# A two-layer transformer block on one core: layer 0's norms split, one key tile a step through DRAM, one copy per Strassen group, and output weight sums in product order

## The chip, the cores and the metric

One core of a Trainium2 chip runs the whole computation in one launch. The metric is the device time of that launch in microseconds (us). Engines: PE (TensorE, matrix products and transposes), DVE (VectorE), ACT (ScalarE), POOL (GpSimd) and SP (SyncE, which here issues nearly all DMAs). Each engine works through its own queue in order; semaphores tie the queues together.

## What is computed

Two layers over x (4 sequences of 256 tokens, 512 wide, fp32), each an attention and a feed-forward part, with a layer norm after each sum:

```python
x = _layernorm(x + _L0_attn_ref(x, ...))   # 32 query heads, 8 key/value heads, head size 16, causal, softmax, biases
x = _layernorm(x + _L0_ffn_ref(x, ...))    # x @ W.T + bias, W = scales * (codes - 128), 512 x 512
x = _layernorm(x + _L1_attn_ref(x, ...))   # 32 query heads, 8 key/value heads, head size 128, causal, bias -slope*sqrt(distance)
x = _layernorm(x + _L1_ffn_ref(x, ...))    # x @ w, w one block of 64 rows repeated 8 times
# _layernorm(x) = (x - mean) / sqrt(var + 1e-5)
```

## The kernel before, in words

Tokens lie in eight tiles of 128 (`tt`), two to a sequence. Both layers run the same software pipeline, `run` (L315): in each turn it begins a step (scores, softmax), calls `fill` (pieces of other work: projections, tails, output products), transposes the probabilities of the step begun `lag` turns earlier, and ends (products with v) the step begun `lag + more` turns earlier. The order within each engine's queue is made from this by a scheduler that places instructions by their dependences; `keep_in_program_order` and `issue_after` pin a few.

**Layer 0.** 64 steps: 4 sequences `b`, 2 query tiles `qt`, 2 groups `h` of key heads, 4 query groups `i`. The eight steps of a sequence with `qt` 0 have one key tile and are called its one-tile half, the eight with `qt` 1 have two key tiles and are its two-tile half. `begin0` (L453) multiplies 32-row slices of qT and kT into a score tile `sc` of two PSUM banks; two such tiles exist, so the scores of a step wait until the exponentials of the step two before have read theirs. DVE adds the causal mask (L467) and takes the negated maximum (L470), ACT makes four exponentials with their sums (L270), DVE takes the reciprocal (L275), and POOL divides (L276). `transpose0` (L483) turns the probabilities, so that keys are on partitions, in one of two ways:

- on PE (`transposed_probabilities`, L286): four 128x128 transposes into a PSUM bank for each key tile, then an ACT copy (L480) into `prT`;
- through DRAM (`transposed_by_blocks`, L294): DVE transposes 32x32 blocks (L300), SP writes them to a DRAM tile `way` with four DMAs (L306) and reads them back into `prT` with one (L310).

`BY_BLOCKS` chooses the steps of the second way, for all their key tiles at once: groups 0 and 2 of a one-tile half, groups 0 and 1 of a two-tile half, except for the one-tile half of sequence 0. `end0` (L501) multiplies with v once all four groups are there (L512). When both `h` are done, `tail0` (L418) is queued: output projection `py` (L422), sum (L424), `layer_norm` (L252: statistics on DVE, the power -0.5 on POOL at L259, the normalisation on DVE at L260), transposes `pt_x` (L266), feed-forward `pf` (L437), second norm, transposes into x2T. Each `yield` ends a piece that one `fill` emits.

**Layer 1.** 64 steps: 8 key/value heads `kv`, 4 sequences, 2 query tiles; lag 1, more 1. The projections (`project1`, L647) and the output products (`outputs1`, `output_products`) are in Strassen's form with seven products in place of eight: `Quarters.early` makes products 1 and 2, `late` the rest; the sums on the left and right sides are POOL's (`left_sums` L591, `right_of` L829). All products go through a ring of three PSUM banks (`bank_m`). `early` copies product 1 out twice:

```python
nc.scalar.copy(C[0, 0], bank)
nc.scalar.copy(C[0, 1], bank)
bank = self.product(2, A[0, 1], Bq[1, 0])
nc.vector.tensor_tensor(C[0, 0], bank, C[0, 0], ALU.add)
```

`output_products` (L894) runs once per head and sequence: product 4, then 1 and 5, 6 and 7, 2 and 3 (PE line L851). Probabilities go through DRAM, but for the last head, whose transposes are on PE and whose `prT` is written in plain order.

Of the kernel before, what the change touches and what calls it, by code (L numbers as in the profile page):

```python
# [59 lines left out]
def block_kernel(  # L60
# [190 lines left out]

    def layer_norm(dst, y, name):  # L252
        st = s0.tile([P, 6], F32, tag="bn", name=f"bn_{name}", bufs=4)
        mv = s0.tile([P, 2], F32, tag="mv", name=f"mv_{name}", bufs=4)
        rs = s0.tile([P, 1], F32, tag="rs", name=f"rs_{name}", bufs=4)
        nc.vector.bn_stats(st, y)
        nc.vector.bn_aggr(mv, st)
        nc.vector.tensor_scalar(rs, mv[:, 1:2], EPS, 1.0, ALU.add, ALU.mult)
        powers.append(nc.gpsimd.tensor_tensor(rs, rs, minus_half, ALU.pow))  # L259
        nc.vector.tensor_scalar(dst, y, mv[:, 0:1], rs, ALU.subtract, ALU.mult)  # L260

# [24 lines left out]
    def transposed_probabilities(name, pr, parts, copy=evacuate):  # L286

        for kt, dst in enumerate(parts):
            pt = bank_t(f"pt_{name}_{kt}")
            for i in range(G):  # L290
                nc.tensor.transpose(pt[:, i, :], pr[:, i, ts(kt, P)], ident)
            copy(dst, pt)

    def transposed_by_blocks(sp, name, pr, nt, dst, bufs):  # L294

        blocks = sp.tile([P, 2, 4, G, 32], F32, tag="blocks", name=f"blocks_{name}", bufs=bufs)
        for kt in range(nt):
# [118 lines left out]
    def tail0(tt, oT):  # L418
# [4 lines left out]
        y = s0.tile([P, D], F32, tag="y", name=f"y_{tt}")  # L423
        nc.vector.tensor_tensor(y, py, x[tt], ALU.add)  # L424
        x1 = s0.tile([P, D], F32, tag="x1", name=f"x1_{tt}")
        layer_norm(x1, y, f"a{tt}")
        yield True
        yield True
# [11 lines left out]
        y2 = s0.tile([P, D], F32, tag="y", name=f"y2_{tt}")  # L440
        nc.vector.tensor_tensor(y2, pf, x1, ALU.add)
        x2[tt] = xp.tile([P, D], F32, tag="x", name=f"x2_{tt}")
        layer_norm(x2[tt], y2, f"b{tt}")
        yield True
        yield True
# [30 lines left out]
    open0 = {}  # L476
    BY_BLOCKS = [(0, 2), (0, 1)]

    def ordered_copy(dst, src):
        nc.scalar.copy(dst, src.rearrange("p n (j q) -> p n j q", q=32))  # L480


    def transpose0(b, qt, h, i, pr):  # L483

        name = f"0_{b}_{qt}_{h}_{i}"
        nt = qt + 1
        if i == 0:
            open0["p", h] = a0.tile(
                [P, 2, G, 4, 4, 32], F32, tag="prT", name=f"prT0_{b}_{qt}_{h}"
            )  # L490
        prT = open0["p", h]
        if (b, qt) > (0, 0) and i in BY_BLOCKS[qt]:
            transposed_by_blocks(a0, name, pr, nt, prT[:, 0:nt, i], 2)
        else:
            copy = evacuate if (b, qt) == (0, 0) else ordered_copy
            transposed_probabilities(
                name, pr, [prT[:, kt, i].rearrange("p j n q -> p n j q") for kt in range(nt)], copy
            )
        return prT
# [37 lines left out]
    def fill():  # L537
# [12 lines left out]
        lag=3,  # L550
        more=2,
    )
# [37 lines left out]

    def left_sums(S, A):  # L591
        nc.gpsimd.tensor_tensor(S[0], A[1, 0], A[1, 1], ALU.add)
        nc.gpsimd.tensor_tensor(S[1], S[0], A[0, 0], ALU.subtract)  # L593
        nc.gpsimd.tensor_tensor(S[2], A[0, 0], A[1, 0], ALU.subtract)
        return nc.gpsimd.tensor_tensor(S[3], A[0, 1], S[1], ALU.subtract)

    class Quarters:
# [15 lines left out]
        def early(self):  # L613

            A, C = self.A, self.C
            bank = self.product(1, A[0, 0], Bq[0, 0])
            nc.scalar.copy(C[0, 0], bank)
            nc.scalar.copy(C[0, 1], bank)  # L618
            bank = self.product(2, A[0, 1], Bq[1, 0])
            nc.vector.tensor_tensor(C[0, 0], bank, C[0, 0], ALU.add)  # L620
            yield True
# [206 lines left out]

    def right_of(kv):  # L829
        if kv not in rights:  # L830
            wo1 = weights1[kv][1]
            Bm = {
                (j, m): wo1[:, 2 * j : 2 * j + 2, ts(m, HALF)] for j in range(2) for m in range(2)
            }
            to = s1.tile([P, 3, 2, HALF], F32, tag="to", name=f"to_{kv}", bufs=1)
            T2_, T3_, T4_ = (to[:, n] for n in range(3))
            T1_ = Bm[0, 1]
            with tc.issue_after(powers[-1].ins):
                nc.gpsimd.tensor_tensor(T3_, Bm[1, 1], Bm[0, 1], ALU.subtract)
                nc.gpsimd.tensor_tensor(T1_, Bm[0, 1], Bm[0, 0], ALU.subtract)  # L840
                nc.gpsimd.tensor_tensor(T2_, Bm[1, 1], T1_, ALU.subtract)
                nc.gpsimd.tensor_tensor(T4_, Bm[1, 0], T2_, ALU.subtract)
            T = T1_, T2_, T3_, T4_
            rights[kv] = Bm, T
        return rights[kv]

# [36 lines left out]
    def outputs1(kv, b, o2):  # L883
        Bm, T = right_of(kv)
        A = {(l, j): o2[:, l, 2 * j : 2 * j + 2, :] for l in range(2) for j in range(2)}
        so = s1.tile([P, 4, 2, P], F32, tag="so", name=f"so_{kv}_{b}", bufs=1)
        S = [so[:, n] for n in range(4)]
        done = left_sums(S, A)
        if merges:
            with tc.issue_after(done.ins):  # L890
                merge()
        return output_products(kv, b, A, S, Bm, T)

    def output_products(kv, b, A, S, Bm, T):  # L894
        (S1, S2, S3, S4), (T1, T2, T3, T4) = S, T
        name = f"{kv}_{b}"
        flat = [kept[b][:, n].rearrange("p a n -> p (a n)") for n in range(2)]
        first = kv == 0
        bank = products(f"po4_{name}", [(A[1, 1], T4)])
        corner = x2[2 * b + 1][:, 0:HALF]  # L900
        nc.vector.tensor_tensor(corner, bank, corner, ALU.add)
        added(flat[0], products(f"po15_{name}", [(A[0, 0], Bm[0, 0]), (S1, T1)]), first)
        yield True
        added(flat[1], products(f"po67_{name}", [(S2, T2), (S3, T3)]), first)
        bank = products(f"po23_{name}", [(A[0, 1], Bm[1, 0]), (S4, Bm[1, 1])])
        nc.vector.tensor_tensor(x2[2 * b], bank, x2[2 * b], ALU.add)
        if kv == NKV - 2:
            merges.append(b)
        yield True

# [32 lines left out]
    def transpose1(kv, b, qt, pr):  # L943
        name = f"1_{kv}_{b}_{qt}"
        nt = qt + 1
        if kv == NKV - 1:
            prT = s1.tile([P, 2, 4, G, 32], F32, tag="prT", name=f"prT_{name}")
            transposed_probabilities(
                name, pr, [prT[:, kt].rearrange("p j h q -> p (j h q)") for kt in range(nt)]
            )  # L950
            return prT
        prT = s1.tile([P, 2, 4, G, 32], F32, tag="prT", name=f"prT_{name}")
        transposed_by_blocks(s1, name, pr, nt, prT[:, 0:nt], 1)
        return prT

    def end1(kv, b, qt, prT):
        o = ps_o.tile([P, G * P], F32, tag="o", name=f"o1_{kv}_{b}_{qt}")
        for kt in range(qt + 1):
            nc.tensor.matmul(  # L959
                o,  # L960
                v1[:, 2 * b + kt, ts(kv, P)],
                prT[:, kt].rearrange("p j h q -> p h j q")
                if kv < NKV - 1
                else prT[:, kt].rearrange("p j h q -> p (j h q)"),
                start=(kt == 0),
# [94 lines left out]
```

## Time and profile before

| What | Value |
| --- | --- |
| Three runs of the kernel | 987.88, 989.89, 992.61 us (median 989.89) |
| The profiled execution | 987.82 us, span 985.9 us |
| Mean granted TensorE clock | 0.980 |
| Busy: PE, DVE, POOL, ACT | 935.1, 620.6, 442.8, 327.3 us |
| First product of layer 1 (p_k, L610) | 294.7 us after the start of the span |
| PE busy, 0 to 300 us and 400 to 900 us | 267.06 of 300 and 493.66 of 500 us |
| DRAM trips: writes of 128 and 64 KB, reads | 176, 160, 84 |

How to read it: the span runs from the first to the last instruction of the core; the time of an execution is a little longer than its span. Rows name engine, line, operation, and out<-in with shapes; a number behind "idle" or in brackets with an arrow is the time that the engine stood before the instruction, and what released it. An fp32 product of the program is two PE instructions; 512 columns start every 0.43 us, 256 every 0.216, 128 every 0.109. PEclk is the share of the clock that PE was granted.

### The profile page before, as it was taken

What the parts mean: (1) busy time and instruction counts of PE and PEld (TensorE: products, weight loads), DVE (VectorE), ACT (ScalarE), POOL (GpSimd) and SP (SyncE); (2) the same over time, 40 slices, a digit from 0 to 9 for tenths busy, and PEclk for the clock granted to TensorE, in tenths of its full rate; (3) what the DMA queues carried; (4) which work ended last, traced back from release to release, by engine and by line L of the source; (5) the groups of instructions that cost most, each with busy time, mean ns of one, the idle gap of its engine ahead of it and who ended that gap; (6) DMA issues with size and microseconds to landing.
All of it is one profiled execution on the core that took longest, in us unless ns stands there. A gap on an engine that the chain in (4) does not pass through costs nothing.

```text
span 985.9 us, 11321 instructions
## 1 busy us (share of the span) xinstructions
PE 935.1 (95%) x3417; PEld 541.9 (55%) x3417; DVE 620.6 (63%) x1291; ACT 327.3 (33%) x1218; POOL 442.8 (45%) x461
## 2 busy tenths in 40 slices
PE   7999889988889999999999999999999999999996
PEld 5645435443334444566666666566666566657652
DVE  3786756766733445855666676566666566666566
ACT  2556454565522001423222222222222222223442
POOL 2364452553426512444543633634534553457732
PEclk9999979998899999999999999999999999999998
DMA  9444343443332010444433444333453434343001
GB/s 264 151 104 114 79 112 74 97 117 76 71 100 85 22 43 4 104 136 120 140 108 95 125 132 110 122 82 114 116 141 86 108 88 135 78 126 88 0 22 64
DMA packets 106817, 97.50 MB, mean 99 GB/s; under 512 B 8197, under 2 KB 77446, under 8 KB 106758
## 3 DMA queue, kind: packets, MB, share of 16 engines
q1 hardware_dynamic: 105942, 95.36, 35.9%
q10 hardware_dynamic: 816, 1.44, 0.5%
q8 instruction: 27, 0.44, 0.2%
q14 instruction: 32, 0.26, 0.1%
HBM read 61.11 MB, written 35.65 MB: 98 GB/s over the span
## 4 chain that ended last, share of the span: by engine, by line
PE 74%; POOL 8%; DVE 8%; ACT 5%; issue 2%; DMA 1%; SPq 0%; POOLq 0%; DVEq 0%; ACTq 0%
PE p_q L610 18%; PE po L851 14%; PE o L959 7%; PE sc L919 7%; PE p_v L610 5%; PE p_k L610 5%; POOL pr L276 4%; ACT pr L270 4%; PE o L512 3%; PE py L815 3%; PE sc L462 3%; DVE blocks L300 2%; PE pq L383 2%; DVE nm L470 2%; PE py L422 2%
## 5 line engine op out<-in xcount | busy, mean ns | idle before, releaser
L270 ACT ACTIVATE pr<-sc,nm 128x256 f32<-128x256 f32 (+1 forms) x512 | 209.0, 419 | 375.4 <-DVE nm L935 272.1
L276 POOL TENSOR_TENSOR pr<-pr,sums 128x512 f32<-128x512 f32 (+1 forms) x128 | 187.8, 1469 | 275.9 <-DVE sums L275 262.4
L300 DVE STREAM_TRANSPOSE blocks<-pr 128x512 f32<-128x512 f32 x128 | 87.5, 698 | 69.1 <-POOL pr L276 69.1
L927 DVE SCALAR_TENSOR_TENSOR sc<-table,sc 128x128 f32<-128x128 f32 (+1 forms) x256 | 86.2, 356 | 34.1 <-PE sc L919 32.1
L270 ACT ACTIVATION_READ_ACCUMULATOR pr<-sc,nm 128x1 f32 x512 | 103.6, 202 | 0.0
L919 PEld LDWEIGHTS sc<-kT,qT 128*128 128x128 f32 x512 | 82.1, 191 | 35.2 <-issue 28.7
L919 PE MATMUL sc<-kT,qT 128*128 128x256 f32 (+1 forms) x512 | 95.4, 327 | 0.0
L959 PE MATMUL o<-prT,v 128*128 128x512 f32 x192 | 92.9, 592 | 0.0
L625 DVE TENSOR_TENSOR qT<-p_q,qT 128x512 f32<-128x512 f32 x96 | 64.4, 685 | 34.1 <-PE p_q L610 33.4
L462 PE MATMUL sc<-kT,qT 32*128 32x256 f32 (+1 forms) x256 | 64.3, 564 | 11.8 <-ACT pr L270 11.6
L935 DVE TENSOR_REDUCE nm<-sc 128x2 f32<-128x512 f32 (+1 forms) x128 | 70.2, 551 | 1.7
L851 PE MATMUL po<-wo,o 128*128 128x256 f32 x224 | 58.0, 381 | 4.0 <-ACT qT L618 4.0
L470 DVE TENSOR_REDUCE nm<-sc 128x4 f32<-128x512 f32 (+1 forms) x64 | 60.6, 948 | 0.7
L610 PE MATMUL p_q<-x2T,ws_q 128*128 128x512 f32 x128 | 60.0, 592 | 0.0
L102 ACT COPY o<-o 128x512 f32<-128x512 f32 x29 | 17.0, 585 | 128.8 <-PE o L959 128.8
L610 PE MATMUL p_q<-xt,ws_q 128*128 128x512 f32 x128 | 57.8, 593 | 1.8 <-POOL ws_q L593 1.8
L467 DVE TENSOR_TENSOR sc<-sc,causal 128x512 f32<-128x512 f32 x64 | 43.9, 687 | 22.9 <-PE sc L462 22.6
L610 PE MATMUL p_q<-x2T,wq 128*128 128x512 f32 x128 | 57.6, 592 | 0.0
L851 PE MATMUL po<-wo,so 128*128 128x256 f32 x224 | 57.5, 379 | 0.0
L512 PE MATMUL o<-prT,v 128*32 128x512 f32 x192 | 53.0, 654 | 2.0 <-issue 2.0
L851 PE MATMUL po<-to,so 128*128 128x256 f32 x224 | 52.9, 379 | 0.0
L851 PEld LDWEIGHTS po<-to,so 128*128 128x128 f32 x224 | 42.6, 190 | 16.9 <-issue 12.2
(160 smaller groups left out, 1406.2 us busy)
## 6 DMA issues: line engine op xcount, KB each, us to landing
way<-blocks SPq DMA_DIRECT2D x176, 128.0 KB, 2.5
prT<-way SPq DMA_DIRECT2D x44, 512.0 KB, 3.7
way<-blocks SPq DMA_DIRECT2D x160, 64.0 KB, 1.8
prT<-way SPq DMA_DIRECT2D x40, 256.0 KB, 2.7
wq<-in_L_attn_w_qkv_dram SPq DMA_DIRECT2D x8, 1024.0 KB, 5.2
wo<-in_L_attn_w_o_dram SPq DMA_DIRECT2D x8, 1024.0 KB, 5.9
wk<-in_L_attn_w_qkv_dram SPq DMA_DIRECT2D x4, 512.0 KB, 4.4
wv<-in_L_attn_w_qkv_dram SPq DMA_DIRECT2D x2, 1024.0 KB, 5.1
```

The lines of the kernel that those rows point to most:

```text
L270: nc.scalar.activation(pr[:, i, 0:w], sc, AF.Exp, bias=nm[:, i : i + 1], accum_out=sums[:, i : i + 1])
L276: nc.gpsimd.tensor_tensor(pr[:, :, 0:w], pr[:, :, 0:w], sums.unsqueeze(2).to_broadcast([P, G, w]), ALU.mult)
L300: nc.vector.transpose(blocks[:, kt].rearrange("p j h q -> p h j q"), pr[:, :, ts(kt, P)].rearrange("p h (j k) -> p h j k", k=32),)
L462: nc.tensor.matmul(sc[:, j, :, 0:w], qT[rows, i, ts(qt, P)], kT[rows, :, 0:w], start=True, stop=True)
L470: nc.vector.tensor_reduce(nm, scf[:, :, 0:w], AX.X, ALU.max, negate=True)
L512: nc.tensor.matmul(o[32 * r : 32 * r + 32, :], v[:, kt, r, ts(e, 32)], prT[:, kt, :, :, 2 * j + e, :], start=(kt == 0 and e == 0), stop=(k ...
L610: nc.tensor.matmul(bank, fixed, moving, start=(c == 0), stop=(c == 1))
L851: nc.tensor.matmul(bank[:, ts(n, HALF)], left[:, c, :], right[:, c, :], start=(c == 0), stop=(c == 1),)
L919: nc.tensor.matmul(sc[:, m, 0:w], qT[:, 2 * j + m, b * S + qt * P : b * S + (qt + 1) * P], kT[:, b * S : b * S + w], start=True, stop=True,)
L927: nc.vector.scalar_tensor_tensor(sc[:, m, 0:w], table[:, 2 * P - w :], slopes[kv * G + 2 * j + m], sc[:, m, 0:w], ALU.mult, ALU.add,)
L935: nc.vector.tensor_reduce(nm[:, 2 * j : 2 * j + 2], sc[:, :, 0:w], AX.X, ALU.max, negate=True)
L959: nc.tensor.matmul(o, v1[:, 2 * b + kt, ts(kv, P)], prT[:, kt].rearrange("p j h q -> p h j q") if kv < NKV - 1 else prT[:, kt].rearrange(" ...
```

## The change

Five edits:

1. `layer_norm` is cut into `norm_factors` (statistics, power) and `normalise`; `tail0` has a `yield` between them, and one fewer behind.
2. Layer 0's probabilities: one key tile, tile 0, of a step goes through DRAM, for every step of the two-tile halves and the even groups of the one-tile halves; tile 1 goes through PE. Not in the one-tile half of sequence 0, nor in the last four steps (sequence 3, `qt` 1, `h` 1), which go through PE altogether. `blocks` is half as large there, with two buffers as before. `more` is 3 in place of 2.
3. `Quarters.early` copies product 1 once, and product 2 is added from that copy.
4. The output weight's four sums are issued between the left sums of the first sequence, and that sequence takes product 4 last.
5. The last head's `prT` is written in the order of the others.

```diff
-    def layer_norm(dst, y, name):
+    def norm_factors(y, name):
...
         powers.append(nc.gpsimd.tensor_tensor(rs, rs, minus_half, ALU.pow))
-        nc.vector.tensor_scalar(dst, y, mv[:, 0:1], rs, ALU.subtract, ALU.mult)
+        return mv[:, 0:1], rs
+
+    def normalise(dst, y, factors):
+        nc.vector.tensor_scalar(dst, y, *factors, ALU.subtract, ALU.mult)
...
-        for kt, dst in enumerate(parts):
+        for kt, dst in parts:
...
-            copy(dst, pt)
+            copy(dst, pt.rearrange("p i (j q) -> p i j q", q=32))
...
-    def transposed_by_blocks(sp, name, pr, nt, dst, bufs):
+    def transposed_by_blocks(sp, name, pr, nt, dst, room):
...
-        blocks = sp.tile([P, 2, 4, G, 32], F32, tag="blocks", name=f"blocks_{name}", bufs=bufs)
+        blocks = sp.tile(
+            [P, room, 4, G, 32], F32, tag="blocks", name=f"blocks_{name}", bufs=2 // room
+        )
...
+        factors = norm_factors(y, f"a{tt}")
+        yield True
         x1 = s0.tile([P, D], F32, tag="x1", name=f"x1_{tt}")
-        layer_norm(x1, y, f"a{tt}")
-        yield True
+        normalise(x1, y, factors)
         yield True
...
-    BY_BLOCKS = [(0, 2), (0, 1)]
...
-        if (b, qt) > (0, 0) and i in BY_BLOCKS[qt]:
-            transposed_by_blocks(a0, name, pr, nt, prT[:, 0:nt, i], 2)
-        else:
-            copy = evacuate if (b, qt) == (0, 0) else ordered_copy
...
+        rest = range(qt + 1)
+        if (0, 0) < (b, qt) and (b, qt, h) < (B - 1, 1, 1) and (qt == 1 or i % 2 == 0):
+            rest = rest[1:]
+            transposed_by_blocks(a0, name, pr, 1, prT[:, 0:1, i], 1)
+        copy = evacuate if (b, qt) == (0, 0) else nc.scalar.copy
+        transposed_probabilities(
+            name, pr, [(kt, prT[:, kt, i].rearrange("p j n q -> p n j q")) for kt in rest], copy
+        )
...
-        more=2,
+        more=3,
...
-    def left_sums(S, A):
+    def left_sums(S, A, between=None):
         nc.gpsimd.tensor_tensor(S[0], A[1, 0], A[1, 1], ALU.add)
+        if between:
+            between()
...
             bank = self.product(1, A[0, 0], Bq[0, 0])
-            nc.scalar.copy(C[0, 0], bank)
             nc.scalar.copy(C[0, 1], bank)
             bank = self.product(2, A[0, 1], Bq[1, 0])
-            nc.vector.tensor_tensor(C[0, 0], bank, C[0, 0], ALU.add)
+            nc.vector.tensor_tensor(C[0, 0], bank, C[0, 1], ALU.add)
...
+        less(T3_, Bm[1, 1], Bm[0, 1])
+        less(T1_, Bm[0, 1], Bm[0, 0])
+        yield True
+        less(T2_, Bm[1, 1], T1_)
+        yield True
+        less(T4_, Bm[1, 0], T2_)
+        yield True
...
+        if b == 0:
+            right = right_sums(kv)
+            next(right)
+            left_sums(S, A, lambda: next(right))
+            next(right)
...
+        order = [four, one_and_five, six_and_seven, two_and_three]
+        if b == 0:
+            order = order[1:] + order[:1]
+        for n, part in enumerate(order):
+            part()
+            if n == 3 and kv == NKV - 2:
+                merges.append(b)
+            if n % 2:
+                yield True
...
-                name, pr, [prT[:, kt].rearrange("p j h q -> p (j h q)") for kt in range(nt)]
+                name, pr, [(kt, prT[:, kt].rearrange("p j h q -> p h j q")) for kt in range(nt)]
```

## The prediction

> **What bounds the kernel now.** First the page: which engine is full where.
>
> ```profile
> span 985.9 us, 11321 instructions
> ...
> PE   7999889988889999999999999999999999999996
> ...
> DVE  3786756766733445855666676566666566666566
> ...
> POOL 2364452553426512444543633634534553457732
> PEclk9999979998899999999999999999999999999998
> ```
>
> A slice is 24.6 us. From slice 13 (320 us, layer 1) PE is full at full clock; in the first twelve (layer 0) it has gaps, and the granted clock dips exactly there. So layer 1 is priced by its few PE gaps, layer 0 by what starves PE. Next the windows by half sequence of layer 0 (columns: window, length, then busy us of PE, weight loads, DVE, ACT, POOL; then PEclk):
>
> ```profile
> 70.70:101.70 31.00, 30.61 (x142) 15.71 (x141) 21.84 (x46) 17.11 (x73) 13.59 (x13) 1.00 0.45 115
> 101.70:142.50 40.80, 34.21 (x137) 15.61 (x136) 28.68 (x51) 18.70 (x72) 18.59 (x14) 0.90 0.40 94
> 142.50:175.30 32.80, 32.75 (x140) 16.05 (x140) 20.13 (x44) 16.93 (x74) 12.26 (x12) 0.92 0.31 81
> 175.30:210.60 35.30, 30.79 (x135) 14.82 (x134) 27.37 (x49) 18.72 (x72) 18.75 (x14) 1.00 0.45 105
> ```
>
> The halves with one key tile (first, third) are full on PE. Those with two key tiles are not, though DVE is busy only 28 of 35 to 41 us: DVE, strictly in order, waits too. The timeline at 112 to 121 shows for whom:
>
> ```profile
> 112.14 1.30 DVE L300 STREAM_TRANSPOSE blocks<-pr 128x512 f32<-128x512 f32 x2 [0.90 <-POOL pr L276]
> ...
> 114.24 1.89 POOL L276 TENSOR_TENSOR pr<-pr,sums 128x1024 f32<-128x1024 f32 x1 [2.14 <-DVE sums L275]
> ...
> 116.09 0.55 POOL L259 TENSOR_TENSOR rs_b<-rs_b,minus_half 128x1 f32<-128x1 f32 x1
> 116.68 0.55 DVE L260 TENSOR_SCALAR x<-y,mv_b,rs_b 128x512 f32<-128x512 f32 x1 [0.92 <-POOL rs_b L259]
> ...
> 120.44 2.08 PE L462 MATMUL sc<-kT,qT 32*128 32x512 f32 x4 [3.45 <-ACT pr L270]
> ```
>
> A block transpose waits for POOL's divide (1.89 us after the reciprocal); the normalise waits for a power queued behind another divide. The next score's maximum is queued behind both, its exponentials come late, their PSUM banks come free late, and PE stands 3.45 us. Then the clock halves, as these windows (same columns) show:
>
> ```profile
> 116.90:120.40 3.50, 0.08 (x1) 0.00 (x0) 3.50 (x6) 1.93 (x8) 0.00 (x0) 0.99 0.01 4
> 120.40:127.10 6.70, 6.67 (x18) 1.83 (x18) 2.68 (x6) 2.41 (x9) 6.10 (x4) 0.50 0.67 157
> ```
>
> Such spells begin at 120, 141, 236 and 257 (6.8 us each) and two half as long at 32 and 274: 34 us, of which about 14 us are lost.
>
> In layer 1 a PE gap looks like this (timeline at 625):
>
> ```profile
> 625.47 1.89 PE L851 MATMUL po<-to,so 128*128 128x256 f32 x8
> ...
> 626.59 0.58 ACT L617 COPY qT<-p_q 128x512 f32<-128x512 f32 x1
> ...
> 627.96 0.61 ACT L618 COPY qT<-p_q 128x512 f32<-128x512 f32 x1
> ...
> 628.62 1.13 PE L851 MATMUL po<-wo,o 128*128 128x256 f32 x4 [1.26 <-ACT qT L618]
> ```
>
> The products need the bank that the second copy still reads.
>
> **The change, part by part.** Orders of the changed program are those in which it is built.
>
> *One copy per Strassen group.* 24 ACT copies of 0.59 us go. ACT is 33% busy, so their 14 us count only where they hold a bank. Eight product matmuls at 0.216 us from 625.47 end at 627.20, PE went on at 628.62: 1.42 us, and the first copy was done at 627.17. This stall appears twice (627, 780); a smaller one of 0.65 us three times (562, 715, 868). Gain 2.8 + 1.9 = 4.7.
>
> *Output weight's sums.* The source interleaves them with the left sums, but in the built POOL queue the four weight sums still stand together ahead of the left sums. What does change is PE: for the first sequence product 4 goes last. Before, it waited for the fourth weight sum (0.70 us, at 561, 713, 867); now product 1 starts at once, and product 5 waits for the first left sum (ending 562.3 by the old times, when PE would come at 561.9): 0.45 us. Gain 3 x 0.25 = 0.75, and most of 0.93 us at 412. Layer 1 in sum: **-6**, between 0 and -10 (PE's and its weight loads' waits for L618 and L842 sum to 15.7, but overlap). The last head group's probabilities are now written permuted: the ordered copy (0.594 us) costs what the plain one does (0.588): nothing.
>
> *One key tile a step.* In the two-tile half, four steps sent two tiles through DRAM and four none; now each of eight sends one. DVE's count is the same (8 x 0.70 us), PE's and ACT's too. What differs is the number of times that DVE waits for a divide. I walk DVE's queue of sequence 2's two-tile half from the end of the maximum of step 0 to that of step 7, each instruction at its row (causal 0.69, maximum 1.21, reciprocal 0.17, block 0.70, y, statistics 0.67 each, normalise 0.55; four exponentials 1.94 after the maximum; divide 1.99 after the reciprocal with its start; power 0.6 behind the divide). A wait is 1.99 less what stands between reciprocal and block. The old queue gives waits of 1.4, 0.8, 0.9, 0.95, 2.0, 0.6, in sum 6.6, and ends after 32.2 us; the trace has 31.5, so the walk can be trusted to a few per cent. The new queue: reciprocal and block stand side by side (2.0), around a maximum (0.85), a normalise behind a divide (1.2), a reciprocal right behind its maximum (1.65), around causal (1.3), around y (1.3), normalise (1.15): 9.45. So **+3** for each of three such halves, and +0.5 in the four DRAM steps left in the fourth: **+9.5** (behind the waiting block stand the next step's causal add and maximum on DVE; for them wait ACT's exponentials, then the score bank, then PE), from 0 (PE's order hides it) to +15 (each wait also starves PE).
>
> SP: 40 trips of five issues take the place of 28, 60 more issues at 0.44 us. A step then takes some 2.2 us of SP in a step of 4 to 5 us. The read of a trip now stands behind three writes of the next step, so its tile lands about 6 to 8 us after its transposes; the o products come three steps, some 13 us, later. Cost 0; without that cover some 2 us per o. In the two-tile halves an issue moves 64 instead of 128 KB and lands in 1.8 instead of 2.5 us.
>
> *more=3.* The o products come one step later. At 234.6 PE stood 2.14 us for a read issued at 233.89; that goes, and the half clock of 236.3 to 243.1 behind it: 2.1 + 2, **-4** (0 to -5.5). The probabilities' and v's buffers are held a step longer: two steps are left before they are wanted again, cost 0.
>
> *The end of layer 0.* The last four steps go through PE: four more tiles, 16 transposes of 0.109 us, 1.7 us, in place of DMA trips. From the last maximum (275.4) to layer 1's first product (294.7) the trace has 19.3 us: o waited for a read until 275.9, ran at half clock, the feed-forward, 16 transposes, then pt_x for a normalise (1.3 us), and only then the last o. In the new PE order the last o stands ahead of that pt_x. From the last maximum, at 29.8 us of the same walk: divide done 33.8; PE meanwhile does transposes, o (3.6), feed-forward (1.7), last transposes to 36.9, copy, o to 41.1, oT, py to 43.5. The trace took 51.0 over the same stretch: **-7.5** (-2 to -10).
>
> *Norms in two pieces.* The normalise moves behind one or two instructions; its wait for the power (3.9 us in all) stays, about 1 us each, as walked above: 0 (-5 to +3). pt_x waits of 1.8 to 1.9 us behind it stay as likely.
>
> *The clock.* The half-clock spells cost some 14 us of layer 0. I leave as many as there are, beyond the one above: 0, from -7 to +10.
> [...]
>
> **Sum.** -6 + 9.5 - 4 - 7.5 = -8 on the profiled 987.8 (span 985.9 and 1.9 around it): 979.8. The median of the runs, 989.9, is 2.1 above that execution, so I add part of it: **981**.
>
> **Rivals.**
> *DVE's waits decide (slower).* In the two-tile halves DVE's queue gets 36 us where PE needs 30. If the added waits fall together, as 1.2 + 1.65 do between steps 2 and 3, PE's gap passes 3 us, and each half gets two half-clock spells of 3.4 us cost: 3 halves x (3 + 4 to 5) = +23, less 6 and 7.5 elsewhere: 998. It decides from about one more spell per half. For it: the 3.45 us gap above. Against it: the window from 175.3 shows gaps of 1.5 to 1.9 us with PEclk 1.00.
> *Evening pays.* PE's own queue hides the new waits, stalls on the scores' banks (15 us in layer 0) shrink by half and with them half of the clock loss: -8 - 9.5 - 3 = 967. For it: DVE and PE have equal work in every step. Against: the walk.
> *Only layer 1 gains*, the end of layer 0 being eaten by the waits and a new spell: 988 in the median. It includes that the reordered sums do nothing, which the POOL queue suggests.
>
> **How the numbers follow.** The sum 0.50 (own range 974 to 988), DVE's waits 0.18, evening 0.20, layer 1 alone 0.12. A difference of 0.5% is about what can be told from no change here. Faster (under 985): 0.50 x 0.75 + 0.20 + 0.12 x 0.1, about 0.59; slower (over 994.8): 0.17; same: 0.24. The range runs from evening to most of the slow case: 965 to 997.
>
> **What would show it.** Right: no wait of po for an ACT copy; DVE's waits for the divide in the first 300 us up from 18.5 to about 28; layer 1 beginning 2 us sooner than 294.7; o in layer 0 never waiting for a read. Wrong: PEclk under 0.9 in more slices of layer 0, or the last o waiting for the last divide for over 4 us more than walked.

## The result, and the profile after

The changed kernel takes 992.98 us (median of 13 runs, 991.16 to 994.48), the kernel before 989.75 (13 runs, 985.06 to 992.61): ratio 1.0039, interval 1.0025 to 1.0053. It is slower, by less than 0.5%; forecast were 981 us and a range of 965 to 997. The profiled execution took 993.61 us, its span is 991.4. Two executions among the experiments below, one of e1 (1014.92 us) and one of g1 (1216.22 us), were slow, at a granted clock of 0.931 and 0.751, and are left out of the ratios and medians. The page of the changed kernel, same lines as before:

```profile
span 991.4 us, 11477 instructions
...
PE   7989979989989999999999999999999999999996
...
DVE  3757766656754345755566666667666666666566
...
POOL 2344443443444611443633534543544453467732
PEclk9889999989899999999999999999999999999998
```

PE is full from slice 13 on as before; the dips of PE and of the granted clock are still all in layer 0, but for the last slice (6 and 8). After the first slice the clock is under 0.9 in four slices of layer 0 (before: three), and PE is busy for under 90% in four (before: six). The stages say where the time came from. Layer 1 (first product to the end of the span) went from 691.2 to 688.5 us, layer 0 from 294.7 to 302.9. In layer 0 I cut at the end of the first maximum of each half sequence. Windows of the changed kernel, sequences 1 and 2, one-tile and two-tile half in turn (columns: window, length, busy us of PE, weight loads, DVE, ACT, POOL; PEclk; DMA share, GB/s):

```profile
82.10:114.10 32.00, 31.50 (x140) 15.13 (x139) 22.52 (x47) 16.30 (x74) 11.99 (x13) 1.00 0.39 100
114.10:153.10 39.00, 32.53 (x137) 16.75 (x134) 26.40 (x46) 18.87 (x69) 19.02 (x13) 0.91 0.36 90
153.10:187.00 33.90, 31.45 (x140) 15.04 (x138) 21.84 (x48) 16.68 (x76) 11.97 (x13) 1.00 0.36 90
187.00:227.40 40.40, 35.50 (x138) 16.82 (x134) 26.47 (x47) 18.91 (x69) 19.09 (x13) 0.84 0.33 82
```

The two-tile halves of sequences 1 and 2 in the kernel before, cut the same way:

```profile
108.00:145.10 37.10, 30.60 (x117) 13.96 (x117) 25.53 (x47) 18.93 (x71) 18.07 (x13) 0.85 0.42 100
179.30:212.80 33.50, 28.96 (x126) 14.00 (x128) 25.55 (x47) 18.85 (x71) 18.03 (x13) 1.00 0.50 121
```

The two-tile halves are now 39 and 40 us long where DVE is busy for 26 and POOL for 19, and part of PE's 33 and 36 busy us is there only because its clock was at 0.91 and 0.84. Cut the same way, the three two-tile halves of sequences 0 to 2 took 28.5, 37.2 and 33.5 us before and 35.0, 39.0 and 40.4 after: +15.2. The one-tile half of sequence 3 went from 30.9 to 27.7, the last half up to layer 1 from 51.0 to 47.8, the rest by -0.6: +8.2 in all for layer 0, -2.8 for layer 1.

DVE's waits in the first 300 us (engine, line, what it waited for: us in total, times, longest), before and after:

```profile
DVE sc L467 <- PE sc L462: 22.6, 18, 3.0
...
DVE blocks L300 <- POOL pr L276: 18.5, 18, 2.1
```

```profile
DVE blocks L306 <- POOL pr L280: 30.0, 24, 2.1
...
DVE sc L475 <- PE sc L470: 9.5, 11, 2.2
```

The waits for the divide rose to 30.0 us (forecast: about 28), those for PE's scores fell by 13: in the changed kernel it is DVE's queue that comes late, and PE that waits for it. That looks like the forecast's slower rival. The experiments show that the waits are not where the price lies.

### The profile page after: what moved, and what is told of

It reads as the page before. It is cut to its first block, busy times and chain, and to the rows that moved or that the text cites. A ratio compares the mean times of both kernels' runs of the same rounds, so it can differ in the third digit from the quotient of the medians.

```text
span 991.4 us, 11477 instructions
## 1 busy us (share of the span) xinstructions
PE 941.6 (95%) x3433; PEld 546.3 (55%) x3433; DVE 620.6 (63%) x1287; ACT 316.3 (32%) x1198; POOL 443.2 (45%) x461
## 4 chain that ended last, share of the span: by engine, by line
PE 74%; POOL 11%; DVE 7%; ACT 3%; issue 2%; DMA 2%; SPq 0%; POOLq 0%; DVEq 0%; ACTq 0%
PE p_q L615 18%; PE po L858 14%; PE sc L945 7%; PE o L985 7%; POOL pr L280 5%; PE p_k L615 5%; PE p_v L615 5%; PE o L515 3%; ACT pr L274 3%; PE py L819 3%; PE sc L470 3%; DVE nm L478 2%; PE pt L295 2%; DVE blocks L306 2%; PE pq L389 2%
## 5 line engine op out<-in xcount | busy, mean ns | idle before, releaser
L945 PE MATMUL sc<-kT,qT 128*128 128x256 f32 (+1 forms) x512 | 95.2, 327 | 0.0
L629 DVE TENSOR_TENSOR qT<-p_q,qT 128x512 f32<-128x512 f32 x96 | 64.6, 686 | 35.6 <-PE p_q L615 34.8
L515 PE MATMUL o<-prT,v 128*32 128x512 f32 x192 | 55.8, 670 | 1.0 <-DMA prT<-way 0.7
L279 DVE RECIPROCAL sums<-sums 128x4 f32<-128x4 f32 x128 | 21.9, 171 | 50.1 <-ACT pr L274 49.8
```

Of the source, the lines that this page charges most:

```text
L515: nc.tensor.matmul(o[32 * r : 32 * r + 32, :], v[:, kt, r, ts(e, 32)], prT[:, kt, :, :, 2 * j + e, :], start=(kt == 0 and e == 0), stop=(k ...
L945: nc.tensor.matmul(sc[:, m, 0:w], qT[:, 2 * j + m, b * S + qt * P : b * S + (qt + 1) * P], kT[:, b * S : b * S + w], start=True, stop=True,)
```

## The experiments

"The changed kernel" is the whole change; each run changes only what is said. Medians vary with the set of runs, so the ratios to the kernel before, taken on the same chip, are what is compared. Stages are those of the profiled execution: layer 0's end, the sum of the two-tile halves of sequences 0 to 2, the sum of the one-tile halves of sequences 1 to 3, the last half up to layer 1, layer 1, and the time at half clock within layer 0.

| Kernel | Ratio (interval) | Layer 0 | Two-tile | One-tile | Last | Layer 1 | Half clock |
| --- | --- | --- | --- | --- | --- | --- | --- |
| before | 1 | 294.7 | 99.2 | 98.0 | 51.0 | 691.2 | 34 |
| changed | 1.0039 (1.0025 to 1.0053) | 302.9 | 114.4 | 93.6 | 47.8 | 688.5 | 44 |
| e1 old routing, more=2 | 0.9974 (0.9955 to 0.9993) | 294.8 | 100.7 | 96.6 | 51.0 | 688.1 | 34 |
| e2 single copy only | 0.9967 (0.9945 to 0.9990) | 299.4 | 98.2 | 102.3 | 51.9 | 687.0 | 48 |
| e3 divide by tile | 0.9971 (0.9948 to 0.9994) | 297.7 | 112.2 | 93.7 | 44.6 | 688.4 | 34 |
| e4 more=2 | 0.9931 (0.9903 to 0.9958) | 289.9 | 99.1 | 95.5 | 48.6 | 688.4 | 34 |
| f1 before, more=3 | 1.0036 (1.0018 to 1.0053) | 301.8 | 111.2 | 93.4 | 50.5 | 691.4 | 38 |
| f2 tail earlier | 1.0096 (1.0067 to 1.0124) | 306.2 | 111.1 | 97.6 | 50.6 | 688.6 | 48 |
| f3 oT on ACT | 0.9979 (0.9958 to 0.9999) | 298.2 | 109.7 | 95.2 | 46.3 | 688.5 | 41 |
| f5 blocks behind maximum | 0.9983 (0.9964 to 1.0002) | 293.7 | 107.1 | 96.7 | 46.5 | 688.4 | 24 |
| g1 projections later | 0.9854 (0.9824 to 0.9883) | 287.5 | 103.0 | 86.6 | 47.9 | 688.7 | 24 |
| g2 more=2, projections earlier | 1.0109 (1.0081 to 1.0137) | 313.4 | 116.6 | 102.8 | 47.1 | 688.5 | 65 |
| f4 more=2, divide, old order | 0.9926 (0.9901 to 0.9950) | 292.6 | 98.9 | 99.4 | 47.7 | 687.3 | 34 |
| g4 later, divide, old order | 0.9817 (0.9786 to 0.9849) | 281.4 | 100.6 | 87.2 | 47.9 | 687.3 | 20 |
| g5 before, more=3, later | 1.0054 (1.0030 to 1.0078) | 299.2 | 111.8 | 90.2 | 51.0 | 691.3 | 38 |
| h2 later, old order | 0.9848 (0.9814 to 0.9883) | 282.4 | 103.2 | 86.5 | 46.4 | 687.6 | 17 |
| h3 later, last four by DRAM | 0.9928 (0.9902 to 0.9953) | 289.2 | 103.2 | 86.6 | 53.5 | 688.6 | 24 |
| i1 g5, pairs 2 and 3 | 1.0110 (1.0076 to 1.0144) | 310.2 | 107.5 | 98.0 | 55.0 | 691.3 | 51 |
| i3 g5, pairs 0 and 3 | 1.0076 (1.0047 to 1.0105) | 303.8 | 108.6 | 93.0 | 55.7 | 691.3 | 44 |
| i4 g5, pairs 0 and 2 | 1.0019 (0.9991 to 1.0047) | 295.6 | 104.7 | 93.1 | 51.8 | 691.3 | 27 |

### Which edit costs

**e1_old_route:** the changed kernel with layer 0's routing and `more` as before.

```diff
...
-        if (0, 0) < (b, qt) and (b, qt, h) < (B - 1, 1, 1) and (qt == 1 or i % 2 == 0):
-            rest = rest[1:]
-            transposed_by_blocks(a0, name, pr, 1, prT[:, 0:1, i], 1)
+        if (0, 0) < (b, qt) and i in [(0, 2), (0, 1)][qt]:
+            rest = []
+            transposed_by_blocks(a0, name, pr, qt + 1, prT[:, 0 : qt + 1, i], 2, 2)
...
-        more=3,
+        more=2,
```

> The changed kernel with the routing of layer 0 as it was before (two key tiles of half the steps through DRAM, the last four steps too, more=2); norms in two pieces, single copy and order of the output products stay. Theory W (waits): one key tile a step makes DVE wait for POOL's divide in every step, and DVE's queue sets the pace of the two-tile halves. Then layer 0 falls back to 294.7 us or up to 2 beside it, DVE's waits of the block transposes for the divide fall from 30.0 to about 18.5 us before 300 us, and with layer 1's 2.75 us the whole is 986 to 988, 0.997 of the kernel before. Rival N (norms): the later normalise delays PE in each tail; then layer 0 stays at 300 us or more and the time at 992 or more.

Measured 0.9974, layer 0 ends at 294.8, the waits for the divide are 15.8 us. So the loss is in the routing with its `more`, and the split norms cost nothing that these runs can tell (rival N falls).

**e2_single_copy:** the kernel before with `nc.scalar.copy(C[0, 0], bank)` left out and the next sum read from `C[0, 1]`.

> The kernel before with one copy per Strassen group alone. If layer 1 lost part of its gain to the order of the output products, layer 1 (from its first product to the end) takes 691.2 - 4.8 = 686.4 us here against 688.45 in the changed kernel, layer 0 stays at 294.7, and the whole is 985, 0.995. If the copies freed less than the stalls showed, layer 1 takes 688.5 or more and the whole is 987 or more.

Layer 1 took 687.0 us: 4.2 gained, of 4.7 forecast. Its layer 0 is the code of before and ended at 299.4 in this execution, with 48 us at half clock in place of 34: layer 0 varies by some 5 us between executions of the same instructions, which is why the ratios decide.

**e3_divide_by_tile:** `divided` multiplies each key tile's 128x512 by itself.

```diff
...
-        nc.gpsimd.tensor_tensor(
-            pr[:, :, 0:w], pr[:, :, 0:w], sums.unsqueeze(2).to_broadcast([P, G, w]), ALU.mult
-        )
+        for t in range(0, w, part):
+            cut = pr[:, :, t : min(t + part, w)]
+            nc.gpsimd.tensor_tensor(
+                cut, cut, sums.unsqueeze(2).to_broadcast([P, G, cut.shape[2]]), ALU.mult
+            )
...
```

> The changed kernel with layer 0's divide cut by key tile: two multiplications of 128x512 (1.04 us each) in place of one of 128x1024 (1.89 us), so that the block transpose of tile 0 need not wait for tile 1's part. Theory W: each of some 25 waits shrinks by up to 0.85 us, DVE's waits for the divide fall from 30.0 to 10 to 16 us, each of the first three two-tile halves gets 3 to 5 us shorter, and layer 0 ends 8 to 15 us earlier: 978 to 985. Rival (PE's own order and PSUM banks set the pace, the waits are only idle time of DVE): layer 0 within 2 us of 302.9; POOL's 0.19 us more per step may even cost: 991 to 996.

DVE's waits for the divide fell by a third, from 30.0 to 19.8 us, yet the two-tile halves only from 114.4 to 112.2. In its profile most of the gain (0.7% over the runs) is at the end of layer 0, where the last divide stands alone on the path (last half 47.8 to 44.6); it had less half clock too (34 us for 44). Theory W is wrong about the halves.

**e4_more2:** the changed kernel with `more=2`.

> The changed kernel with more=2 in place of 3. Theory W: the products with v a step earlier make no difference to DVE's waits (30 us, two-tile halves of 34 to 40 us as in the changed kernel); the one-tile half of sequence 3 gets up to 3 us longer: 993 to 997. Rival M (the delay of one step is what lengthens layer 0, since tails and the next half's work come later): layer 0 falls to 297 us or less, 985 to 988.

0.9931: 1.08% less than the changed kernel, 10.7 us. W expected it slower; rival M is right about the edit. And this kernel has the waits too:

```profile
DVE blocks L306 <- POOL pr L280: 28.3, 26, 2.1
DVE sc L475 <- PE sc L470: 18.6, 16, 2.9
```

28.3 us of waiting for the divide in the first 300 us, nearly as with `more=3`, and two-tile halves of 99.1 us, as before the change (99.2). One key tile a step does add the waits, and beside `more=2` they cost nothing. Against e1 the kernel is 0.43%, 4.3 us, faster. So the result splits into three, each good to about 3 us: single copy, order of the products and norms -2.6 us, routing -4.3, `more=3` +10.7. They are steps from one kernel to the next, so that they add up to the whole is no test of them, and the last is what `more=3` costs beside the new routing.

### Why more=3 costs

**f1_before_more3:** `more=3` on the kernel before.

> The kernel before with more=3 alone. The comparison of the changed kernel with its more=2 form left 11 us on more=3, where the prediction had a gain of 4. Theory Q (queue between two maxima): with more=3 the tail's second norm comes a step later, and DVE's queue then holds two block transposes, y, statistics and the normalise between two maxima of one half; a maximum that comes late makes exponentials, banks and PE late. Here the built queue has only one block between those maxima, since the two-tile transposes stand elsewhere: layer 0 gets 2 to 6 us longer than 294.7, 990 to 995. Rival S (more=3 is bad only through the shorter reads of one key tile): layer 0 within 2 us of 294.7 or 2 to 4 us shorter, as predicted for the wait at 234.6: 985 to 988.

1.0036: it costs there too, and the time is in theory Q's range; the one-tile half of sequence 3 got 4.9 us shorter, as forecast, and the two-tile halves 12 longer. The whole is some 3.5 us, a third of what it costs beside the new routing. What does the queue do? The stretch between two maxima in sequence 2's two-tile half of the changed kernel, whose ends are at 194.0 and 202.7 (timeline, DVE and POOL of it; the last three rows show who waits behind it):

```profile
194.89 0.71 DVE L306 STREAM_TRANSPOSE blocks<-pr 128x512 f32<-128x512 f32 x1 [0.88 <-POOL pr L280]
195.52 0.65 DVE L448 TENSOR_TENSOR y<-pf,x 128x512 f32<-128x512 f32 x1
...
196.21 0.69 DVE L257 BATCH_NORM_STATS2 bn_b<-y 128x6 f32<-128x512 f32 x1
...
197.23 0.47 DVE L392 TENSOR_SCALAR qT<-pq,bcol 128x256 f32<-128x256 f32 x1
...
198.70 1.26 POOL L397 TENSOR_TENSOR x<-x,bo_b 128x512 f32<-128x512 f32 x1
198.77 1.48 DVE L264 TENSOR_SCALAR x<-y,mv_b,rs_b 128x512 f32<-128x512 f32 x1 [1.07 <-POOL rs_b L260]
...
200.17 0.70 DVE L306 STREAM_TRANSPOSE blocks<-pr 128x512 f32<-128x512 f32 x1
...
200.80 0.66 DVE L475 TENSOR_TENSOR sc<-sc,causal 128x512 f32<-128x512 f32 x1
...
201.50 1.23 DVE L478 TENSOR_REDUCE nm<-sc 128x4 f32<-128x1024 f32 x1
...
202.84 0.47 ACT L274 ACTIVATE pr<-sc,nm 128x256 f32<-128x256 f32 x1 [5.14 <-DVE nm L478]
...
204.82 2.08 PE L470 MATMUL sc<-kT,qT 32*128 32x512 f32 x4 [2.68 <-ACT pr L274]
...
211.77 0.69 DVE L100 COPY oT<-o 128x512 f32<-128x512 f32 x1 [3.42 <-PE o L515]
```

Two blocks, the tail's sum, statistics and normalise, and a projection's qT: 8.7 us between two maxima. ACT stood 5.1 us for the second, PE 2.7 for ACT, and the half clock came at 204.1; an o that ran for the most part at half clock then kept DVE's copy to oT, queued ahead of a maximum, waiting for 3.4 us. Three runs took single pieces out.

**f2_tail_earlier:** the first `if tt < NTT - 1: yield True` of `tail0` left out.

> The changed kernel (more=3) with the first empty piece of each tail left out, so that from the first transposes on every piece of a tail falls into the same turn as with more=2. Theory Q: the built queue of DVE still has two blocks, y, statistics and the normalise between two maxima, twice per two-tile half (reciprocal, block, y, statistics, block, normalise): the half of sequence 2 stays at 36 to 40 us and the time at 988 to 993. Rival T (the turn in which the tail's pieces fall is what counts): that half falls to 31 to 34 us and the time to 981 to 985.

1.0096, slower than either expected; that half took 39.6 us, with a stretch of 8.9 and one of 9.2 us: rival T falls.

**f3_oT_on_ACT:** in `end0`, `nc.scalar.copy` in place of `evacuate` for oT.

> The changed kernel with layer 0's copies of o into oT all on ACT, other copies where they were. Theory Q: only the wait of DVE for o goes (8.4 us in three waits, the longest 3.4, ahead of a maximum): 2 to 5 us less than the changed kernel, 988 to 991, and the long intervals with two blocks between maxima stay. Rival O (the copy of o ahead of a maximum is the cause of the 11 us): 980 to 984.

0.9979, 0.6% under the changed kernel: some 6 us, a little more than expected; the stretches of 8.9 and 8.4 us stay.

**f5_blocks_behind_max:** each block transpose pinned behind the next step's maximum.

```diff
...
-            transposed_by_blocks(a0, name, pr, 1, prT[:, 0:1, i], 1)
+            step = ((2 * b + qt) * 2 + h) * G + i
+            with tc.issue_after(maxima[step + 1].ins):
+                transposed_by_blocks(a0, name, pr, 1, prT[:, 0:1, i], 1)
```

> The changed kernel (more=3) with one thing pinned: each block transpose of layer 0 stands behind the maximum of the next step on DVE. No work is added or left out. Theory Q: no interval between two maxima holds two blocks any more; each two-tile half gets 2 to 5 us shorter, the waits of DVE for the divide fall from 30 to under 22 us, layer 0 ends 6 to 12 us earlier: 980 to 986. Rival (the queue order is a consequence, PE's late scores are what counts): layer 0 within 2 us of 302.9, 990 to 995.

0.9983: about half of the gain that theory Q expected, and the long stretches still take 8.1 and 8.0 us with one block in them. Order within the stretch is a part, not the cause. Nor is one long stretch: the same half of the kernel before has two, of 7.1 and 9.6 us, but short ones beside them, and from the first maximum to the last it takes 31.6 us, the changed kernel 39.0. What stands in a stretch follows PE's order, in the built program, for a two-tile half (sc = scores of group h and i, T = transposes of a step, the rest by name):

```
e4 (more=2):      sc00 pt_x T o sc01 pf sc02 pq T sc03 pq T sc10 pt_x T o sc11 py T sc12 pv T sc13
changed (more=3): sc00 T sc01 pt_x o sc02 pf pq T sc03 pq T sc10 T sc11 pt_x T o sc12 py pv T sc13
```

With `more=2` feed-forward (pf) and queries (pq), and output projection (py) and values (pv), have a score step between them. `more=3` ends an o one turn later, its tail follows, and pf lands on pq, py on pv: two pieces of other work, with their DVE parts, between the same two score steps, and nothing but transposes in other turns. (f2 did not take this apart: in its PE order pf stands away from pq, but beside an o, and py still meets pv.) The projections' turns are set by a table of empty turns (`ROOM`, L356), which was left as it was. That is theory A, and it can be tried both ways, with no work added.

**g1_projections_later**

```diff
-    ROOM = [(0, 0, 0, 0, 0, 0), (0, 0, 0, 1, 0, 3), (2, 2, 0, 2, 0, 2)]
+    ROOM = [(0, 0, 0, 0, 0, 0), (1, 0, 0, 1, 0, 3), (3, 2, 0, 2, 0, 2)]
```

> The changed kernel (more=3) with the hand-written room of the projections one turn larger at its start, so that the projections of the next sequence come one turn later too. No work is added or left out. Theory A (alignment): more=3 moved the tails by one turn into the turns of the projections, so that feed-forward and queries (pf, pq) and output projection and values (py, pv) fall between the same two score steps on PE and DVE; apart again, the longest interval between two maxima falls from 8.7 to under 7 us, each two-tile half from 35 to 40 us to 31 to 34, and the time to 978 to 984. Rival (more=3 costs by itself, by what it holds longer): 989 to 994.

973.84 us in the median, 0.9854: 1.8% under the changed kernel, more than expected. The two-tile halves were expected at 31 to 34 and took 30.2, 35.6 and 37.2, two of them longer than theory A said. They gained 11.4 in sum; the one-tile halves, where py had met pq, gained 7.0 (93.6 to 86.6), and there was 20 us less of half clock. The same stretch of the queue here, 7.2 us (timeline):

```profile
187.28 0.55 POOL L260 TENSOR_TENSOR rs_b<-rs_b,minus_half 128x1 f32<-128x1 f32 x1
187.36 0.71 DVE L306 STREAM_TRANSPOSE blocks<-pr 128x512 f32<-128x512 f32 x1 [0.95 <-POOL pr L280]
...
188.00 0.67 DVE L475 TENSOR_TENSOR sc<-sc,causal 128x512 f32<-128x512 f32 x1
188.57 0.53 DVE L264 TENSOR_SCALAR x<-y,mv_b,rs_b 128x512 f32<-128x512 f32 x1
189.01 1.22 DVE L478 TENSOR_REDUCE nm<-sc 128x4 f32<-128x1024 f32 x1
```

The normalise waits for nothing: block and causal add stand where its wait was, and the qT is gone to the next turn.

**g2_projections_earlier:** `more=2` and a table with one empty turn fewer, `(0, 0, 0, 0, 0, 3), (1, 2, 0, 2, 0, 2)`.

> The opposite: the changed kernel with more=2 and the projections' room one turn smaller at the start, so that the same pieces meet although more is 2. Theory A: pf and pq, and py and pv, fall between the same two score steps, intervals of 8.5 us or more appear, the two-tile halves take 35 to 39 us, and the time is 988 to 996 where more=2 alone had 982. Rival: within 3 us of 982.

1.0109, 1.8% over e4: stretches of 8.9 and 8.5 us, 65 us at half clock. So the pieces that meet cost 1.8% with either `more` (g2 against e4, the changed kernel against g1), and apart, `more=3` costs nothing: g1 is 0.8% faster than e4. But `more=2` with the later table was not run. That a later table helps whatever `more` is, for another reason, is therefore not excluded; that in the two slower of these four kernels the pieces stand together, and in the two faster ones apart, is what PE's orders show.

### The other terms, and the best version

**f4_more2_split_old_order:** e4 with e3's divide, and `right_of`, `outputs1`, `output_products` as before.

> The changed kernel with more=2, layer 0's divide cut by key tile, and the output products with their weight sums in the old order (single copy stays). Layer 1 takes 687.0 us as with the single copy alone, 1.4 less than in the changed kernel, if the order of the products is what lost that; 688.4 if it is the last head's order or the copies. Layer 0 ends at 284 to 290: the divide's cut takes 2 to 5 us off the end of layer 0 and less off the halves. 975 to 981.

Layer 1 took 687.3: 1.1 of the changed kernel's loss was the order of the products. The whole, 0.9926, is above what was expected and no better than e4: the waits for the divide went from 28.3 to 21.1 us and the two-tile halves from 99.1 to 98.9.

**g4_all:** g1 with the same two edits.

> more=3 with the projections a turn later, the divide cut by key tile and the old order of the output products. Theory A: as with more=2 and the same two edits, within 4 us, and below it by the wait for the read in the one-tile half of sequence 3 (2 to 3 us): 972 to 980. If more=3 costs by itself: 982 or more.

970.96 us, 0.9817: the lowest of all, 2.2% under the changed kernel, though its interval overlaps that of g1.

**h2_aligned_old_order:** g1 with the old order alone.

> The changed kernel with the projections a turn later and the output products with their weight sums in the old order: the order alone, at an equal layer 0. Layer 1 takes 687.3 us against 688.7, the whole 1.4 less than 974.8, 972 to 975. If the order cost nothing: layer 1 at 688.5 or more.

Layer 1 gains 1.1 us of the 1.4 expected; the whole (975.0) can't be told from g1.

**h3_last_four_by_dram:** g1 without `and (b, qt, h) < (B - 1, 1, 1)`.

> The changed kernel with the projections a turn later, and the last four steps of layer 0 through DRAM like the other steps of two key tiles. It prices the end of layer 0, which was forecast at 7.5 us less and came 3.2 less. If PE's way is worth what is left of it: from the first maximum of the last half to layer 1's first product 49.5 to 53 us instead of 47.9, and the whole 1.5 to 5 us longer, 976 to 980. If it is worth nothing: 973 to 976.

981.25 us; the last half takes 53.5 in place of 47.9. Sending the last four steps through PE is worth 5.6 us there and 7 by the ratios, more than expected.

**g5_before_aligned:** `more=3` and g1's table on the kernel before.

> The kernel before with more=3 and the projections a turn later, nothing else. Theory A says that the meeting of tails and projections made more=3 cost 3.5 us on the kernel before, whatever way the probabilities go: apart, the time falls from 993.5 to 978 to 986, and the rest of the way to the 974.8 of the changed kernel with the same room is the single copy (3 to 4 us), the one-tile routing and the end of layer 0. If the gain of the room needs one key tile a step: 988 or more.

1.0054, and two-tile halves of 111.8 us: nothing gained in them. Theory A as I had put it, whatever way the probabilities go, is wrong. Three runs moved the steps whose two tiles go through DRAM, `BY_BLOCKS[1]`, from groups (0, 1) to (2, 3), (0, 3) and (0, 2).

**i1_pairs_in_groups_2_3**

> The kernel before with more=3 and the projections a turn later, as before it (995.6 us), and the two-tile steps that go through DRAM moved from groups 0 and 1 to groups 2 and 3. In the trace of the former, pairs of block transposes stood with y, statistics and the normalise between two maxima (7.8 us), and PE had o, pt_x and eight transposes of one step in one turn (5.1 us). Theory U (unevenness: what a turn holds on DVE or PE in sum sets its length, whichever piece it is): here PE's eight transposes leave the turns of o, and one pair leaves the norm's: two-tile halves of 33 to 36 us in place of 35 to 39, 984 to 990. Rival V (the way of one tile a step is needed by itself): 993 to 998.

**i3_pairs_in_groups_0_3**

> The same with groups 0 and 3. Theory U: no block transpose is left between the maxima around either normalise (intervals there of 6 to 6.7 us), but PE keeps o, pt_x and eight transposes in one turn and DVE gets four blocks in another: halves of 34 to 37 us, 986 to 992. Rival V: 993 to 998.

**i4_pairs_in_groups_0_2**

> The same with groups 0 and 2: PE's eight transposes leave the turn of o, DVE keeps three to four blocks in the turns of the norms (intervals of 7.5 to 8.5 us). Theory U: halves of 35 to 38 us, 989 to 996, between the other two and the kernel with groups 0 and 1. Rival V: 993 to 998 for all three alike.

1.0110, 1.0076 and 1.0019. All three shorten the two-tile halves (107.5, 108.6, 104.7 for 111.8), as theory U has it, but i1 and i3 lose more elsewhere: the last half grows from 51.0 to 55. Only i4 is within U's range of times; i3 is in that of rival V, i1 in neither. So the table's shift pays 18 us with one key tile a step and nothing with the pairs in groups 0 and 1 (1.0036 without it, 1.0054 with it). The three other placements were run with the shift alone, and none is faster than the kernel before. Why `more=3` costs 3.5 us with the pairs, and whether another table would serve them, stays open.

## Why the prediction was wrong

It forecast -8 us on the profiled execution; the two executions differ by +5.8. Of its signs of being right two came (no matmul of po waits for an ACT copy any more, and DVE waits 30.0 us for the divide) and two did not: layer 1 began 8.2 us later, and an o still waited for a read.

- **more=3, "-4 (0 to -5.5)": the step that failed.** Its mechanism was there: o waits for a read once, for 0.7 us, in place of 2.1, and the one-tile half of sequence 3 lost 3.2 us. But I asked only which buffers are held longer and said "cost 0". I did not ask what follows the o: the tail starts a turn later and meets the projections, whose turns are fixed by a table. Measured: +10.7 us, and moving the table by one turn takes 18 us off (g1). With the old routing `more=3` costs 3.5 us and the table gives nothing back (f1, g5), so the meeting is the account for the changed routing only.
- **One key tile a step, +9.5.** The 28 us of waits came (30.0). But the walk went through a queue that was built with `more=3` and booked what it found to the routing. It gave +3 for each half; from the first maximum to the last those of sequences 0, 1 and 2 grew by 5.3, 3.0 and 7.5. The DVE waits of the last sum to 13.7 us where I walked 9.45: the 3.4 us for an o at half clock was not in the walk, nor was 0.9 us more for one normalise. With `more=2` nearly as many waits cost nothing (e4: 28.3 us, halves of 99.1 for 99.2), which the evening rival had assumed; that PE's queue had other work there is argued. A sum of an off-path engine's waits is not a price.
- **The end of layer 0, -7.5.** Measured -3.2. The change of way is worth 5.6 to 7 (h3). I had walked PE's feed-forward and output projection at half their length, 1.7 us each; the rows have four program matmuls of 0.86 in each:

```profile
290.29 3.70 PE L444 MATMUL pf<-wfT,x1T 128*128 128x512 f32 x8
...
299.41 3.70 PE L428 MATMUL py<-wop,oT 128*128 128x512 f32 x8
```

  Both stand between the last maximum and layer 1: +3.5 us of the 3.8 by which that stretch (17.5) exceeds the walk (13.7).
- **Layer 1, -6.** The single copy gave 4.2 of 4.7. The order of the products, counted as about -1.3, cost 1.1: POOL's queue and PE's row of the changed kernel at 569 to 575 (timelines) show the wait that I left out.

```profile
570.22 0.72 POOL L595 TENSOR_TENSOR so<-o 128x256 f32<-128x256 f32 x1
570.90 0.73 POOL L599 TENSOR_TENSOR so<-o 128x256 f32<-128x256 f32 x1
571.58 0.73 POOL L598 TENSOR_TENSOR so<-so,o 128x256 f32<-128x256 f32 x1
```

```profile
571.00 1.13 PE L858 MATMUL po<-wo,so 128*128 128x256 f32 x4 [0.34 <-POOL so L595]
572.37 1.99 PE L858 MATMUL po<-to,so 128*128 128x256 f32 x8 [0.24 <-POOL so L598]
```

  Product 4 of the kernel before, at the same place:

```profile
561.69 1.13 PE L851 MATMUL po<-to,o 128*128 128x256 f32 x4 [0.54 <-POOL to L842]
```

  Product 5 waits for the first left sum, as forecast, and product 6 for another that POOL builds third: by PE's issue rates 0.51 and 0.41 us of lost time, where the old order lost 0.70 once. That product 4, taken first, gave POOL time for them is argued, not tried.
- **The clock, 0.** In the two profiled executions layer 0 was at half clock for 44 us against 34; by PE's issue rates that lost 18.5 us against 13.8, +4.7. Over the runs there is no such difference: the thirteen of the changed kernel had a mean granted clock of 0.975 to 0.983, median 0.980, 22 runs of the kernel before, taken with h3, 0.973 to 0.982, median 0.977. So 0 was right for the medians, and the clock does not explain them. No run of the changed kernel shows the -7 at the end of the term's range.
- **Norms in two pieces, 0:** right, as far as e1 can tell.

The slower rival saw the direction, with +23 us for the halves where +15.2 were measured, and its two half-clock spells a half came (two, two and three). It got a chance of 0.18; what it named as the cause, the waits that one key tile a step adds, was not the cause.

## What to carry to other kernels

When a change moves a stage by one turn of a software pipeline, write down which pieces then share a turn with it on each engine, and shift everything that is placed by hand against it: here that was worth 18 us of 990, more than all the edits, though with the old routing it was worth nothing. Read a walk of one engine's queue as lengths, and ask which edit put an instruction there, by walking the version without that edit too. Undo edits one at a time even where the whole moves little: here it was -2.6, -4.3 and +10.7 us.

## What the runs showed of the hardware

- **The granted clock changes on a grid.** In the clock records of the two profiles, the 6 half-clock spells in layer 0 of the kernel before and the 9 of the changed kernel begin on multiples of 3.41 us counted from one origin in each (to 0.01 of a step; 0.85 and 2.72 us after the start of the span) and last one or two steps. Half clock went with how busy PE had been within a step: by its issue rates, from the first clock record (at 14.5 and 13.0 us) through layer 0 and the 20 us behind it, each of the 9 steps at full clock in which PE was issuing for at most 0.38 of the time was followed by half clock, and none of the 131 in which it was issuing for over 0.63; between the two both happened. It took no single long gap there: in the kernel before, the step from 253.4 to 256.9 has waits of PE of 1.81 us (before 255.86) and 0.85 us (before 257.37) and PE issuing for 0.26 of the time, and half clock followed. The runs of e2 go from 980.9 us at a granted clock of 0.982 to 988.7 at 0.974; that where the gaps fall among the steps makes this spread was not tested. In the changed kernel the gap of 2.68 us before 204.82 (its row is shown above) was only 2.0 us old when the clock fell, behind a step with PE issuing for 0.30 of the time, and this window followed:

```profile
204.10:210.90 6.80, 6.08 (x18) 2.63 (x20) 3.30 (x5) 4.52 (x16) 3.13 (x2) 0.50 0.39 112
```

- **A step of PE transposes alone kept the full clock.** From 282.6 to 286.0, one step of the grid, PE of the changed kernel issued nothing but transposes, for 0.46 of the time:

```profile
282.63 1.07 PE L295 MATMUL pt<-ident,pr 128*128 128x128 f32 x8 [0.28 <-ACT prT L296]
283.65 0.63 PE L270 MATMUL pt_x<-ident,x 128*128 128x128 f32 x4
285.71 1.09 PE L295 MATMUL pt<-ident,pr 128*128 128x128 f32 x8 [1.43 <-POOL pr L280]
```

  PEclk was 1.00 in this step and in the next (286.0 to 289.4), as it was over 16 transposes in a row of the kernel before (282.84 to 285.0). Had the transposes been idle time to the clock, the step would have stood beside the three at full clock in which PE was issuing for under 0.2 (from 116.9 and 270.5 in the kernel before, from 129.0 in the changed kernel), and half clock followed all three.
- **A normalise took longer where a POOL sum had begun first.** The normalise of 128x512 takes 0.55 us, but 1.48 where POOL's `x<-x,bo_b` (1.26 us) had begun 0.07 us earlier (198.77 in the timeline above, and again at 125.81): it ends 0.3 us after POOL's does. In the kernel before one took 2.02 us at 298.52, beside a POOL sum of 1.80 us that had begun 0.06 us earlier. Where DVE began first, at 77.92 in the changed kernel, it took 0.51 and POOL's divide, over an overlap of 0.26, 2.02 in place of 1.89.
